# Table steps later in the slot, scatters and fetch ahead of the gathers, adding moved into the next projection

## The chip, the core and the metric

The kernel runs on one core of one Trainium2 chip. A core has five engines that run side by side, each with its own queue of instructions: TensorE (PE) multiplies matrices into PSUM, VectorE (DVE) and ScalarE (ACT) do elementwise work and reductions, GpSimd (POOL) does small operations and issues the indirect transfers here, and SyncE (SP) issues the other transfers. Transfers run on 16 DMA engines that all queues share. The metric is device time in microseconds (us) of one execution; lower is better. Before the change it is 2427.53 us, the median of three runs (2426.61 to 2428.74).

## The reference

32 batches of a 512 x 1024 matrix x go through two layers, each with a residual and a layer norm over the 1024 nodes. Layer 0 is attention over nodes whose score is a sum of two numbers per node, followed by a projection with `adj`; layer 1 multiplies with `adj * adj`.

```python
def _L0_gnn_ref(x, wq, wk, wm, bm):
    q = jnp.einsum('c,bcn->bn', wq, x)
    k = jnp.einsum('c,bcn->bn', wk, x)
    scores = q[:, None, :] + k[:, :, None]
    scores = jnp.where(scores > 0, scores, NEG_SLOPE * scores)
    att = jax.nn.softmax(scores, axis=-1)
    agg = jnp.einsum('bcn,bmn->bcm', x, att)
    out = jnp.einsum('oc,bcm->bom', wm, agg) + bm[None, :, None]
    return jax.nn.relu(out)
...
W = support * kernel
out = jnp.einsum('bnf,nm->bmf', x, W)
out = out + bias
...
x = _layernorm(x + _L0_gnn_ref(x, L0_gnn_wq, L0_gnn_wk, adj, L0_gnn_bm), axis=-1)
x = _layernorm(x + _L1_gnn_ref(x, adj, adj, L1_gnn_bias), axis=-1)
```

(`_L1_gnn_ref` is called with `adj` as both `support` and `kernel`.)

## The kernel before

**The method.** The kernel never forms the 1024 x 1024 attention. exp of a leaky score is exp(q + k) where the sum is positive and exp(0.01 (q + k)) elsewhere. So if the rows z = x^T wm^T are sorted by q, the numerator for one node is one prefix sum and one suffix sum over the sorted rows, each with its weights, cut where q + k changes sign. Per batch b this goes in steps:

- `project(b, nt, part)` (L221, L229): z for 128 nodes at a time into a PSUM tile `zp`, in two halves of eight matmuls each; after the second, ScalarE copies it to `zrow`, of which there is one for all batches. Column 0 of `zrow` is q, the last column k.
- `spread(b)` (L237, L241): q along the free axis in every partition (`qb`, copied to `qs`).
- `place(b, nt)` (L262, L266) on VectorE: the rank of each node by comparing with all q. `send(b, nt)` (L271) on POOL: an indirect transfer that scatters 128 rows of `zrow` to a table `td` in DRAM by rank. `order` is `place` and `send`. There are two tables, one for even and one for odd b.
- `count(b, nt)` (L296) on ScalarE: how many q lie on the positive side for each node; `share(b)` (L304 to L314) makes the row index `idx` and factors from it. `top(b)` (L289, L290) on VectorE: the largest q.
- `fetch(b)` (L324, L329) on SP: eight transfers bring the sorted rows back into `zs`, nine blocks j of two groups of 60 rows. There is one `zs`.
- `weigh(b, part)` (L344 on ScalarE, L349 on VectorE): the weights `w` and the triangular matrices `lw`.
- `table(b, step)`, nine steps (L363 to L377): TensorE makes the prefix sums of one block and the suffix sums of another in the PSUM tile `tp`; ScalarE copies them to `ts` (L368); the last row of each is carried into the next block by a one-row copy, one on POOL (L372) and one on ScalarE (L374), so a step needs the carry of the step before; SP writes the sums to the table `td` (L377).
- `pick(b, mt)` (L391) on POOL: an indirect transfer gathers, for 128 nodes, one row of 3 x 514 floats at `idx` into `g`, of which there is one for all batches.
- `shares` (L411 to L418), `scale` (L427, ScalarE), `gain` (L435, VectorE): the normalised weights, and the weighted sum of the three parts, in place in `g`. The texts call the last two the adding. `shares(b)` without bounds reads all eight gathers.
- `turn(b, ot)` (L470, L474): TensorE transposes the sums to channels by nodes and ScalarE applies bias and relu into `y`; `join` (L481, L444) adds x and makes the statistics on VectorE; `root` (L452, L453) on POOL, `shift` (L459) on VectorE and `apply` (L464) on ScalarE finish the layer norm.
- `layer1(b, mt, h)` (L492): `adj * adj` times `y`; `stats1` (L517, L444) adds the bias and makes statistics; again `root`, `shift`, `apply`; `store` (L522) writes the result. `layer1g` (L507) is the same grouped otherwise, for the first and last batches.

**The order.** The instructions are recorded under a manual schedule: each engine runs its own in the order in which the functions are called, and an instruction that waits holds all behind it in its queue. `begin` and `opening` fill the pipeline, `slot(s)` runs for s = 1 to 29, and `end` empties it. A slot works on four batches: `new` = s + 2 is projected, scattered and fetched; `mid` = s + 1 has its tables made and is gathered; s itself goes through `turn`, `join` and layer 1; `old` = s - 1 is finished and stored.

The slot before has two stages. In eight rounds z = 0 to 7, PE alternates half projections of `new`, table steps of `mid` (two per round, z = 0 to 4) and the transposes of s (z = 1 to 4). The gathers of `mid` are called at z = 4. After `spread(new)` come eight steps h = 0 to 7 of layer 1 of s; beside them VectorE ranks `new` and POOL scatters it (h = 0 to 2), SP fetches it (h = 3), and the adding of `mid` runs from h = 4 into z = 0 of the next slot.

**Buffers.** The PSUM pool `mm` has three tiles of 1024 floats per partition that `zp`, `qb`, `op` (of `turn`) and `o` (of layer 1) share in the order of their calls; `tp` has one tile of its own. `zs`, `g` and `zrow` are single. `ts` has two tiles, `x` twelve (three batches).

Of the kernel before, what the change touches and what calls it, by code (L numbers as in the profile page):

```python
# [23 lines left out]
def gat_gcn_resnorm_kernel(  # L24
# [356 lines left out]
    def bare(b):  # L381

        for i, j in ((0, NB - 1), (1, 0)):
            nc.gpsimd.memset(zs[i * G : i * G + 1, j, 1:ZW], 0.0)

# [164 lines left out]
    def begin():  # L550
# [14 lines left out]
        weigh(0, 0)  # L565
        spread(1)
        weigh(0, 1)
        for z in range(NT):
            project(2, z, 0)
            if 2 * z < NB:  # L570
                table(0, 2 * z)
            if z < NT // 2:
                order(1, 2 * z)
            project(2, z, 1)
            if 2 * z + 1 < NB:
                table(0, 2 * z + 1)
            if z < NT // 2:
                order(1, 2 * z + 1)
            if z == NT // 2:
                bare(0)  # L580
                for mt in range(NT):
                    pick(0, mt)
                top(1)
                fetch(1)
            if z >= NT // 2:
                for nt in (2 * z - NT, 2 * z - NT + 1):
                    count(1, nt)
# [3 lines left out]
    def opening():  # L591

        weigh(1, 0)
        place(2, 0)
        weigh(1, 1)
        table(1, 0)
        table(1, 1)
        place(2, 1)
        shares(0, 0, NT // 2)
        scale(0, range(NT // 2))  # L600
        gain(0, range(NT // 2))
        table(1, 2)
        table(1, 3)
        place(2, 2)
        shares(0, NT // 2, NT)
        scale(0, range(NT // 2, NT))
        gain(0, range(NT // 2, NT))
        table(1, 4)
        table(1, 5)
# [8 lines left out]
        apply(0, 0, CT - 1)  # L618
        for nt in range(NT):
            if nt >= 3:  # L620
                place(2, nt)
            send(2, nt)
            count(2, nt)
        top(2)
        bare(1)
        fetch(2)
        for mt in range(NT):
            pick(1, mt)
# [7 lines left out]
        for mt in range(2):  # L636
            shift(1, 0, mt)
            apply(1, 0, mt)
        weigh(2, 0)
        shares(1)  # L640
        scale(1, range(NT))
        gain(1, range(NT // 2 + 1))

    def slot(s):

        new, mid, old = s + 2, s + 1, s - 1
        for z in range(NT):
            step, ot = 2 * z, z - 1
            project(new, z, 0)
            if step < NB:  # L650
                table(mid, step)
            if 0 < ot < CT:
                root(0, s, ot - 1)
            if z == 0:
                if s > 1:
                    root(1, old, CT - 2)
                weigh(mid, 1)
                gain(s, range(5, NT))
            project(new, z, 1)
            if 0 < ot < CT:  # L660
                turn(s, ot)
            if step + 1 < NB:
                table(mid, step + 1)
            if z == 0:
                stats1(old, CT - 1)
                shift(1, old, CT - 2)
            if ot == 0:
                turn(s, ot)
            if ot == CT - 1:
                for mt in range(3):  # L670
                    pick(mid, mt)
            if z == 1:
                root(1, old, CT - 1)
            if 0 <= ot < CT:
                join(s, ot)
            if z == 1:
                apply(1, old, CT - 2)
                shift(1, old, CT - 1)
            if ot == CT - 1:
                root(0, s, ot)  # L680
                for mt in range(3, NT):
                    pick(mid, mt)
            if ot == CT:
                shift(0, s, CT - 1)
                apply(0, s, CT - 1)
            if z == 2:
                share(mid)
            if z == 3:
                apply(1, old, CT - 1)
            if z < CT:  # L690
                store(old, z)
            if new + 1 < B and 2 <= z < 2 + CT:
                load(new + 1, z - 2)
        spread(new)
        for h in range(CT * NH):
# [9 lines left out]
            if h == 3:  # L705
                fetch(new)
            if h == 4:
                stats1(s, 1)
                root(1, s, 1)
                shares(mid)  # L710
                shift(1, s, 0)
                shift(1, s, 1)
            if h == 5:
                scale(mid, range(NT // 2))
                gain(mid, range(NT // 2))
                apply(1, s, 0)
                apply(1, s, 1)
            if h == 6:
                bare(mid)
                weigh(new, 0)  # L720
            if h == 7:
                scale(mid, range(NT // 2, NT))
                stats1(s, 2)
                gain(mid, [NT // 2])

    def end():

        s, mid, old = B - 2, B - 1, B - 3
        table(mid, 0)
        weigh(mid, 1)  # L730
        gain(s, range(5, NT))
        table(mid, 1)
        root(1, old, CT - 2)
        table(mid, 2)
        stats1(old, CT - 1)
        root(1, old, CT - 1)
        share(mid)
        for ot in range(CT):
            turn(s, ot)
            table(mid, 3 + ot)  # L740
# [4 lines left out]
        shift(1, old, CT - 2)  # L745
        shift(1, old, CT - 1)
        layer1g(s, range(CT - 1), 0)
        table(mid, CT + 3)
        layer1g(s, range(CT - 1), 1)
        table(mid, CT + 4)  # L750
        apply(1, old, CT - 2)
        apply(1, old, CT - 1)
        for mt in range(CT):
            store(old, mt)
        layer1g(s, range(CT - 1), 2)
        layer1g(s, range(CT - 1), 3)
        for mt in range(NT):
            pick(mid, mt)
        for mt in range(CT - 1):
# [73 lines left out]
```

## Time and profile before

| What | Value |
|---|---|
| median of 3 runs | 2427.53 us (2426.61 to 2428.74) |
| the profiled execution | 2426.41 us, span 2424.7 us |
| VectorE busy | 1623.8 us, 67% of the span |
| ScalarE busy | 1472.4 us, 61% |
| POOL busy | 1028.4 us, 42% |
| SP's DMA queue | 276.65 MB, 38.0% of 16 engines' span |
| POOL's DMA queue (scatters and gathers) | 269.52 MB, 29.5% |
| granted TensorE clock | 0.978 mean |

The span is cut by the page into 40 slices. The first rows show each engine's busy share in tenths:

```profile
PE   8965999999999999999999999999999999999975
DVE  3274766677766667766667776666777666777665
PEclk9977999999999999999999999999999999999987
```

A slice is about 61 us. PE is at 9 (90% or more) in all but the first four and the last two. The chain that ended last lies to 74% on PE. In the page's groups a line such as "L492 PE MATMUL o<-y,adj_sb" names the line of the kernel, the engine, the operation and the tiles, written on the left of the arrow and read on its right. In timelines the first number is the start in us, the second the length, and brackets hold the engine's idle time before it and what ended that idle time.

### The profile page before, as it was taken

How to read it: one execution, taken by the hardware profiler on the slowest of the kernel's cores; microseconds unless marked ns; L12 is line 12 of the kernel's file. 1: busy time of each engine (PE TensorE's matmuls, PEld its weight loads, DVE VectorE, ACT ScalarE, POOL GpSimd, SP SyncE). 2: the span in 40 equal slices, each digit the busy share in tenths (PEclk: the TensorE clock that was granted, in tenths of full speed). 3: DMA queues.
4: the chain of work that ended last, by engine and by line, in shares of the span. 5: the costliest groups of instructions: out<-in, count | busy, mean ns of one | idle time of the engine just before them, and what ended most of it. 6: DMA issues, size and time to landing. Idle time of an engine off the chain costs nothing.

```text
span 2424.7 us, 30847 instructions
## 1 busy us (share of the span) xinstructions
PE 2305.3 (95%) x9744; PEld 1441.6 (59%) x9744; DVE 1623.8 (67%) x3250; ACT 1472.4 (61%) x2214; POOL 1028.4 (42%) x1353
## 2 busy tenths in 40 slices
PE   8965999999999999999999999999999999999975
PEld 7633666665666665566666556666566666656532
DVE  3274766677766667766667776666777666777665
ACT  2563666666666756666666656675666666666633
POOL 1432445334444434444533444543444443344431
PEclk9977999999999999999999999999999999999987
DMA  6556776667777666777766777676677776677641
GB/s 239 156 190 194 250 257 246 213 211 235 251 247 257 231 204 222 246 253 248 250 210 218 237 245 252 247 235 205 227 242 259 249 245 209 223 238 250 215 172 69
DMA packets 176835, 548.67 MB, mean 226 GB/s; under 512 B 26304, under 2 KB 26304, under 8 KB 176672
## 3 DMA queue, kind: packets, MB, share of 16 engines
q1 hardware_dynamic: 117600, 276.65, 38.0%
q0 software_dynamic: 57344, 269.52, 29.5%
q8 instruction: 77, 1.26, 0.2%
q14 instruction: 86, 0.70, 0.1%
q10 hardware_dynamic: 1728, 0.53, 0.1%
HBM read 338.17 MB, written 208.43 MB: 225 GB/s over the span
## 4 chain that ended last, share of the span: by engine, by line
PE 74%; DMA 8%; ACT 5%; issue 4%; DVE 4%; POOL 4%; SPq 2%; POOLq 0%; ACTq 0%; DVEq 0%
PE o L492 30%; PE zp L221 26%; PE tp L363 11%; PE op L470 4%; DMA x<-in_x_dram 3%; POOL g L391 2%; PE o L507 2%; DMA g<-td,idx 2%; DMA zs<-td 2%; ACT zrow L229 1%; ACT y L464 1%; SPq L377 1%; ACT v L464 1%; DVE g L435 1%; ACT ts L368 1%
## 5 line engine op out<-in xcount | busy, mean ns | idle before, releaser
L221 PE MATMUL zp<-wmT,x 128*128 128x257 f32 x4096 | 976.5, 388 | 0.0
L221 PEld LDWEIGHTS zp<-wmT,x 128*128 128x128 f32 x4096 | 757.5, 191 | 205.7 <-issue 91.9
L492 PE MATMUL o<-y,adj_sb 128*128 128x512 f32 x1856 | 801.3, 592 | 0.0
L492 PEld LDWEIGHTS o<-y,adj_sb 128*128 128x128 f32 x1856 | 351.8, 191 | 430.0 <-issue 423.1
L372 POOL COPY zs<-ts 1x513 f32<-1x513 f32 x256 | 204.2, 798 | 754.8 <-ACT ts L368 754.5
L435 DVE SCALAR_TENSOR_TENSOR g<-g,ra 128x512 f32<-128x512 f32 x512 | 390.7, 789 | 32.6 <-ACT g L427 23.6
L391 POOL DMA_INDIRECT g<-td,idx x256 | 290.3, 1134 | 271.3 <-DMA x<-in_x_dram 168.7
L363 PE MATMUL tp<-zs,lw 128*64 128x257 f32 x2304 | 325.8, 403 | 57.5 <-POOL zs L372 45.7
L262 DVE SCALAR_TENSOR_TENSOR lt<-qs,zrow,first 128x1024 int8<-128x1024 f32 x256 | 327.8, 1281 | 27.8 <-ACT qs L241 26.8
L271 POOL DMA_INDIRECT td<-zrow,ranki x256 | 273.1, 1067 | 123.3 <-issue 70.8
L296 ACT ACTIVATE sg<-qs,kc 128x1024 int8<-128x1024 f32 x256 | 294.0, 1148 | 7.9
L481 DVE TENSOR_TENSOR y<-y,x 128x1024 f32<-128x1024 f32 x128 | 156.8, 1225 | 177.0 <-ACT y L474 176.8
L464 ACT ACTIVATE y<-y,nb,rs 128x1024 f32<-128x1024 f32 x128 | 158.5, 1238 | 179.7 <-DVE nb L459 178.0
L363 PEld LDWEIGHTS tp<-zs,lw 128*64 128x64 f32 x2304 | 146.4, 139 | 194.2 <-POOL zs L372 94.2
L368 ACT COPY ts<-tp 128x514 f32<-128x514 f32 x288 | 167.9, 583 | 151.1 <-PE tp L363 140.8
L229 ACT COPY zrow<-zp 128x514 f32<-128x514 f32 x256 | 146.7, 584 | 152.1 <-PE zp L221 135.9
L459 DVE SCALAR_TENSOR_TENSOR nb<-mv,rs 128x1 f32<-128x1 f32 x256 | 35.8, 150 | 298.9 <-POOL rs L453 291.7
L414 ACT ACTIVATE ac<-s 128x8 f32<-128x8 f32 (+2 forms) x35 | 7.4, 213 | 290.5 <-DVE s L413 290.5
L427 ACT ACTIVATE g<-g,ra 128x512 f32<-128x512 f32 x256 | 163.5, 710 | 32.2 <-DVE ra L418 32.2
L517 DVE TENSOR_TENSOR v<-o,bias_bc 128x1024 f32<-128x1024 f32 x127 | 154.5, 1217 | 23.6 <-PE o L507 23.1
L464 ACT ACTIVATE v<-v,nb,rs 128x1024 f32<-128x1024 f32 x127 | 152.8, 1227 | 27.3 <-DVE nb L459 27.3
L444 DVE BATCH_NORM_STATS2 st<-y 128x6 f32<-128x512 f32 x256 | 164.7, 685 | 4.4
(75 smaller groups left out, 1641.7 us busy)
## 6 DMA issues: line engine op xcount, KB each, us to landing
x<-in_x_dram SPq DMA_DIRECT2D x128, 512.0 KB
out_dram<-v SPq DMA_DIRECT2D x127, 512.0 KB
td<-ts SPq DMA_DIRECT2D x512, 120.5 KB
zs<-td SPq DMA_DIRECT2D x64, 602.3 KB
zs<-td SPq DMA_DIRECT2D x64, 240.9 KB
zs<-td SPq DMA_DIRECT2D x96, 120.5 KB
td<-ts SPq DMA_DIRECT2D x64, 96.4 KB
td<-zs SPq DMA_DIRECT2D x8, 514.0 KB
```

What stands on the lines that cost most here:

```text
L221: nc.tensor.matmul(zp[:, h, 0:CE], xb[ct][:, nt * P : (nt + 1) * P], wmT[:, ct, h * CE : (h + 1) * CE], start=(ct == 0), stop=(ct == CT - 1),)
L229: nc.scalar.copy(zrow[:, nt, :].rearrange("p (h c) -> p h c", h=2), zps.pop((b, nt))[:, :, 0:CE])
L262: nc.vector.scalar_tensor_tensor(lt, qs, zrow[:, nt, 0:1], first[:, o : o + N], ALU.subtract, ALU.is_lt, accum_out=rank[:, nt : nt + 1],)
L271: sc = nc.gpsimd.indirect_dma_start(out=td[:, :], out_offset=bass.IndirectOffsetOnAxis(ap=ranki[:, nt : nt + 1], axis=0), in_=zrow[:, nt, ...
L296: nc.scalar.activation(sg, qs, AF.Sign, bias=kc[:, nt : nt + 1], accum_out=sgn[:, nt : nt + 1])
L363: nc.tensor.matmul(tp[i * G : (i + 1) * G, h, 0:CE], lt[:, i, j, :], zs[:, j, h * CE : (h + 1) * CE], start=True, stop=True,)
L368: nc.scalar.copy(ts.rearrange("p (h c) -> p h c", h=2), tp[:, :, 0:CE])
L372: nc.gpsimd.tensor_copy(zs[0:1, to, 1:ZW], ts[0:1, 1:ZW])
L391: nc.gpsimd.indirect_dma_start(out=gs[b][:, mt, :], out_offset=None, in_=tds[b].rearrange("(s u) c -> s (u c)", u=3), in_offset=bass.Indir ...
L435: nc.vector.scalar_tensor_tensor(u, g[:, k, i, 1 : C + 1], ra[:, k, i : i + 1], u, ALU.mult, ALU.add)
L464: nc.scalar.activation(t, t, AF.Identity, bias=nb, scale=rs)
L492: nc.tensor.matmul(op[:, h * H : (h + 1) * H], w1[:, ct, mt * P : (mt + 1) * P], yt[ct][:, h * H : (h + 1) * H], start=(ct == 0), stop=(ct ...
```

## The change

The edit touches `begin`, `opening`, `slot` and `end`, and takes out `bare`, which zeroed two carry rows that nothing else writes. No instruction's shape changes; the functions are called in another order.

- **Tables.** In a slot the nine steps of `mid` are called from z = 4 on, two per round, and the ninth after the last projection; `weigh(mid)` is called at z = 2 (before: one part at h = 6 of the slot before, one at z = 0).
- **Gathers.** `pick(mid)` is called at h = 3 of layer 1, after the scatters of `new` and `root(1, s, 0)` on POOL, just ahead of SP's `fetch(new)` in the calls (before: at z = 4, ahead of the scatters).
- **Adding.** `shares`, `scale` and `gain` of s are called at z = 0 to 3 (before: from h = 4 of the slot before to z = 0).
- **Layer norms and stores.** `shift`, `apply`, `store` of `old` move to z = 0 to 2; two `turn`s move to z = 6; two loads of x come after `spread`.
- **Opening and end.** In `opening`, three scatters of batch 2 go ahead of the turns, the gathers of batch 1 ahead of the other five and of the fetch; the adding runs one tile at a time between table steps. `end` follows the same pattern, and the last slot begins the tables of the last batch at h = 6.

The diff, cut to its core:

```diff
-    def bare(b):
-
-        for i, j in ((0, NB - 1), (1, 0)):
-            nc.gpsimd.memset(zs[i * G : i * G + 1, j, 1:ZW], 0.0)
...
     def opening():
...
-        for ot in range(CT):
+        for k in range(NT // 2, NT):
+            scale(0, [k])
+            gain(0, [k])
+            if k % 2:
+                table(1, 2 + k // 2)
+        for nt in range(3):
+            send(2, nt)
+        for ot in range(CT):
             turn(0, ot)
...
         apply(0, 0, CT - 1)
+        for mt in range(NT):
+            pick(1, mt)
+        for nt in range(3, NT):
+            place(2, nt)
+            send(2, nt)
         for nt in range(NT):
-            if nt >= 3:
-                place(2, nt)
-            send(2, nt)
             count(2, nt)
         top(2)
-        bare(1)
         fetch(2)
-        for mt in range(NT):
-            pick(1, mt)
...
     def slot(s):
+        tz = NT // 2
         for z in range(NT):
-            step, ot = 2 * z, z - 1
+            step = 2 * (z - tz)
             project(new, z, 0)
             if z == 0:
                 stats1(old, CT - 1)
+                shares(s)
+                shift(1, old, 1)
+                shift(1, old, 2)
+                scale(s, range(NT // 2))
+            if step >= 0:
+                table(mid, step)
+            if z == 6:
+                root(0, s, 1)
+                turn(s, 2)
+            project(new, z, 1)
+            if z == 0:
+                root(1, old, CT - 1)
+                apply(1, old, 1)
+                gain(s, range(2))
+                store(old, 0)
+                store(old, 1)
             if z == 1:
+                gain(s, range(2, NT // 2))
+                scale(s, range(NT // 2, NT))
+                apply(1, old, 2)
+                store(old, 2)
+            if z == 2:
                 shift(1, old, CT - 1)
+                weigh(mid, 0)
+                weigh(mid, 1)
+                gain(s, range(NT // 2, 6))
+                apply(1, old, CT - 1)
+                store(old, CT - 1)
+            if z == 3:
+                gain(s, range(6, NT))
+                share(mid)
+            if z == 5:
+                root(0, s, 0)
+            if z in (4, 5):
+                turn(s, z - 4)
+            if z == 6:
+                turn(s, 3)
+            if step >= 0:
+                table(mid, step + 1)
+            if z in (4, 5):
+                join(s, z - 4)
+            if z == 6:
+                join(s, 2)
+                root(0, s, 2)
+                join(s, 3)
+                root(0, s, 3)
+            if z == 7:
                 shift(0, s, CT - 1)
                 apply(0, s, CT - 1)
...
+        table(mid, NB - 1)
         spread(new)
+        if new + 1 < B:
+            for ct in (2, 3):
+                load(new + 1, ct)
         for h in range(CT * NH):
             layer1(s, h // NH, h % NH)
...
             if h == 3:
+                for mt in range(NT):
+                    pick(mid, mt)
                 fetch(new)
             if h == 4:
                 stats1(s, 1)
                 root(1, s, 1)
-                shares(mid)
                 shift(1, s, 0)
-                shift(1, s, 1)
-            if h == 5:
-                scale(mid, range(NT // 2))
-                gain(mid, range(NT // 2))
                 apply(1, s, 0)
-                apply(1, s, 1)
             if h == 6:
-                bare(mid)
+                stats1(s, 2)
+                root(1, s, 2)
+            if h == 6 and new == B - 1:
                 weigh(new, 0)
+                weigh(new, 1)
+                table(new, 0)
...
     def end():
...
-        layer1g(s, range(CT - 1), 2)
-        layer1g(s, range(CT - 1), 3)
         for mt in range(NT):
             pick(mid, mt)
+        for ct in range(CT):
+            layer1g(s, range(CT - 1), ct)
```

## The prediction

> **What bounds the kernel now.** First the page's busy row, then the busy time per stretch for three windows of one slot's length, then the timeline of TensorE and VectorE where the program starts.
>
> ```profile
> PE 2305.3 (95%) x9744; PEld 1441.6 (59%) x9744; DVE 1623.8 (67%) x3250; ACT 1472.4 (61%) x2214; POOL 1028.4 (42%) x1353
> ```
>
> ```profile
> 334.00:406.00 72.00, 71.12 (x304) 44.52 (x304) 50.50 (x100) 45.60 (x69) 32.89 (x43) 1.00 0.70 232
> 1000.00:1072.00 72.00, 71.43 (x306) 44.61 (x305) 50.39 (x102) 45.95 (x69) 32.21 (x44) 1.00 0.72 235
> 1800.00:1872.00 72.00, 71.84 (x312) 44.84 (x309) 50.91 (x103) 46.20 (x70) 31.94 (x42) 1.00 0.70 235
> ```
>
> Columns: length, then busy of PE, PEld, DVE, ACT, POOL, then clock, DMA share, GB/s. In the slots PE is busy 71.1 to 71.8 of 72 us at full clock. So nothing can be won in a slot but some tenths; what idles lies in the opening and the end. L492 starts at 262.85 in slot 1 and at 2270.37 in slot 29: (2270.37 - 262.85) / 28 = 71.70 us per slot.
>
> The opening holds one passage in which the order is what the change makes of every slot: the scatters first (POOL 170.7 to 181.9), then fetch and gathers together, then the adding.
>
> ```profile
> 183.09 1.06 POOL L391 DMA_INDIRECT g<-td,idx  x1 [0.16 <-issue]
> ```
>
> ```profile
> 183.69 0.69 SPq L324 DMA_DIRECT2D zs<-td  x2
> 184.42 3.06 SPq L329 DMA_DIRECT2D zs<-td  x6
> ```
>
> ```profile
> 212.85 0.17 DVE L411 TENSOR_TENSOR s<-g,kc 128x8 f32<-128x8 f32 x1 [15.19 <-DMA g<-td,idx]
> ...
> 215.35 7.57 DVE L435 SCALAR_TENSOR_TENSOR g<-g,ra 128x512 f32<-128x512 f32 x10 [0.79 <-ACT g L427]
> 222.84 1.15 DVE L349 TENSOR_TENSOR lw<-tri,w 128x448 f32<-128x448 f32 x2
> 223.91 4.79 DVE L435 SCALAR_TENSOR_TENSOR g<-g,ra 128x512 f32<-128x512 f32 x6
> ```
>
> ```profile
> 220.97 1.98 PE L363 MATMUL tp<-zs,lw 128*64 128x257 f32 x8 [18.04 <-POOL zs L372]
> ```
>
> The reader sees: with fetch and gathers at once, the last gather lands 212.85 - 183.09 = 29.7 us after the first is issued; DVE waits 15.2 us for it and PE 18.0 us. By stretches the DMA share is 1.02 to 1.05 from 188 to 208: the engines are full. In a slot of before it is otherwise: gathers go at 1044.98, land by about 1067, the scatters at 1060 to 1070.6, the fetch at 1073 to 1086, each nearly alone, and L411 finds its gathers there (1071.70, 0.17 us wait).
>
> [...]SP's fetch doesn't wait behind POOL's gathers but shares with them; the trace agrees (29.7 us for both). [...]ScalarE and VectorE run their queues strictly in order, so a waiting instruction holds all behind it; the trace agrees (ACT idle 16.12 us before L414 at 213.46). [...]here L363 takes 1.98 us after the 18 us wait, 1.09 otherwise.
>
> **The change, part by part.** Times from the start of layer 1 (L492) in a slot; before, that stage takes 262.85 to 290.32 = 27.5.
>
> 1. Gathers of `mid`. They move from z = 4 (7 us ahead of layer 1) to h = 3, on POOL behind 8 scatters and root(1,s,0). VectorE sets the pace: places start at 1.24 and come each 1.39 us (1053.58, 1054.98, ...), so 12.4; stats1 to 15.1 (1067.5 - 1052.34); root 0.9: 16.0. First gather about 16.6 (POOL idles 0.3 to 2.7 us between root and gather, 1049.7 to 1052.4). SP's fetch starts at about 15.5 (in the beginning the last scatter goes at 57.83 and SP's fetch at 60.62: 2.8 later). Both together 29.7; 0.7 less as the fetch starts earlier, 1.4 more as store(old,0), 0.5 MB at about 0.37 MB/us, falls in. The last gather lands at L = 47.0. From below: gathers 8 x 128 x 6168 B = 6.32 MB at 381 GB/s (stretch 1061:1066), 16.6 us, and fetch 2.06 MB at 232 (1076:1081), 8.9: 25.5, with 2 us to the first packet 43. From above, a POOL gap of 2.7 and the store in full: 50.5.
> 2. What waits. shares(s) stands in z = 0 on DVE, i.e. at 27.5, and all of g is needed: DVE waits about 17 us. Behind it on ACT stand scale and the copy of zp for z = 0; with three PSUM tiles PE gets through z = 0 to 2 (10.4 us, to 38) and stops. From L: gains start at +2.5 (212.85 to 215.35); 8 of 0.757: +8.55. The next DVE instruction is lw of weigh, whose w is behind scale (4 x 0.64), zrow 0.6, apply 1.24, zrow 0.6, scale 2.56, apply 1.24, zrow 0.6 and 2 pairs of exponentials (0.69 each) on ACT from L + 1.75: +12.5, lw to +13.6. Then 8 gains more: +19.7; the last transpose of turn(s,0): L + 20.2 = 67.2.
> 3. PE from there to the next layer 1: half projection 1.74 us, 1.94 after a table; table 1.02; turn 0.87, 1.02 after a table; qb 1.16. Table 1.02; z = 5 6.79; z = 6 7.61; z = 7 with tables 6, 7 and 8 6.94; qb 1.16: 23.5.
> 4. New waits at the tail. Tables 7 and 8 are neighbours with no projection between; a table frees the next one after ts 0.6 and the POOL row 0.6 (1023.65 to 1025.06): 1.45 idle. And root(0,s,3) stands ahead of table 6's row on POOL and needs join(s,3), while apply(0,s,2) stands ahead of table 6's ts on ACT: from the start of z = 6, relu 7.8, adds and statistics to 12.9, root to 13.85, row 14.5, against 12.5 where PE wants table 7: 2.0. Together 3.5. Half clock after the waits: 2.0.
> 5. Saved in the slot: qb's wait for zrow (0.9) and two half projections after a table (2 x 0.2); both are in 3. bare's two POOL memsets (1.09) were in no chain: nothing. Nor do the other moves count: loads 2 and 3 (1 MB) now stand on SP ahead of the fetch, but run in the first 5 us of layer 1 while VectorE still makes ranks; stores 1 to 3 wait on ACT for the adding and hold only table writes that come later; share, root and shift of layer 1 lie in VectorE's and POOL's idle time. If the gathers were on time, these would still be hidden.
>
> A slot is 67.2 + 23.5 + 3.5 + 2.0 = 96.2: 24.5 more than 71.7, 28 times (slots 2 to 29): +686.
>
> 6. Beginning and opening: PE's waits of 6.49 + 18.04 in slot 1 go, since tables come four projections later; adding in opening runs one by one with scale, without the place between (about 5 us less). But gathers(1) now stand ahead of scatters 3 to 7 and the fetch: scatters at about 176 to 183 behind 6.3 MB, fetch to about 202, the last gains 210, turn(1,0) 211, + 29 = 240 against 262.85. -23.
> 7. End: gathers(30) land 47 us after the last layer 1 begins; half of them serve the first shares, but w of batch 31 needs the fetch (44) and stands ahead on ACT. Gains end at about 63 against 40 (2304.05 + 4.66 - 2270.37 and neighbours): +23. Tables 7 and 8 leave layer1g: -3. Gathers(31) earlier: DVE's stats1 is late there anyway (L411 0.69 us wait): 0. +20.
>
> Sum against the profiled execution, 2426.41 (span 2424.7): 2426 + 686 - 23 + 20 = 3109. The median shown, 2427.53, is 1 us over it: 3110.
>
> **The rivals.** (a) Gathers win against the fetch: alone they took about 19.5 us, so L = 36 and 85.2 a slot: 28 x 13.5 = 378, about 2800. For it: 6168-byte packets move faster than 2056-byte ones; against: the opening, where both ended late. (b) Gathers are hidden and only the tail counts: 74.0 (70.5 of work, 3.5 waits), +2.3: 2427 + 64 - 23 = 2468. Against: gathers would have to land by 27, and POOL can't issue them before 16. (c) The other side, faster: the opening's wait goes and the slots stay full at 71.7, since the nine tables in a row have their rows ready and gathers land in time: 2427 - 23 = 2404. It decides if L is under 27 us and the tail under 0.8 us (23 / 28). For it: that wait is real, 24.5 us; against: 16.6 plus 16.6 us of gather bytes alone is 33. (d) Worse: stores, loads and half clock add 8 us more per slot: 3335.
>
> **How the numbers follow.** Forecast 0.80, (a) 0.09, (b) 0.04, (c) 0.03, (d) 0.04. The unknowns per slot: L -3.8 / +3.5, half clock -2 / +0.5, tail -2 / +1, chain of the adding 0.8; as roots of squares -4.8 / +3.8, so 2975 to 3215. For the cases beside it I take 2900 to 3250. 0.2% is about what a measurement of this kernel tells from no change. Faster 0.03 (c), same 0.01, slower 0.96.
>
> **What would show it.** After: slots of about 96 us; DVE waiting some 17 us at shares for the DMA of g; PE idle some 12 us before the fourth projection (ACT zrow) and again at the transposes (DVE g); DMA share near 1 for some 27 us from the middle of layer 1; tables 7 and 8 waiting for POOL. Wrong if shares starts within 2 us of stats1, or if PE's share stays over 93%.

## The result, and the profile after

The changed kernel takes 3109.79 us (median of 4 runs, 3105.65 to 3110.58) beside 2428.14 us for the kernel before (4 runs): a ratio of 1.280, 95% interval 1.278 to 1.283. The profiled execution has a span of 3108.9 us. First the page of the kernel after: the header, the busy row, TensorE's 40 slices, and one line of the table of groups (busy, mean ns, then the idle time before them and what ended most of it).

```profile
span 3108.9 us, 30419 instructions
...
PE 2449.3 (79%) x9744; PEld 1531.4 (49%) x9744; DVE 1625.5 (52%) x3257; ACT 1466.8 (47%) x2215; POOL 943.1 (30%) x1291
...
PE   8787797777977878877887777887777977779765
...
L221 PE MATMUL zp<-wmT,x 128*128 128x257 f32 x4096 | 1063.3, 416 | 381.0 <-ACT zrow L229 381.0
```

VectorE and ScalarE are busy as long as before (VectorE 1625.5 us against 1623.8), PE runs the same 9744 matmuls, but is busy 144 us longer: in parts of the run its granted clock is 0.5, half of full speed, called half clock below (the mean is 0.887, before 0.978). What is new is above all idle time: from the fifth slice on TensorE is mostly at 7 or 8 tenths where it was at 9. The last line names the largest piece of it: the projection waited 381.0 us for ScalarE's copies of earlier projections.

The slots give the size. Layer 1 (L487 here, L492 before) starts at 242.3 in slot 1 and at 2934.7 in slot 29, so a slot lasts (2934.7 - 242.3) / 28 = 96.16 us, against 71.70 before: 28 x 24.46 = +685. The part up to slot 1 is 20.5 us shorter (262.85 to 242.3), the part from slot 29 on 19.9 longer (154.3 to 174.2). 685 - 20.5 + 19.9 = 684 us, the difference of the spans. Over these 28 slots TensorE is busy 76.19 us of a slot and idle 19.97, before 71.08 and 0.61: of the 24.5 us, 19.4 are idle time and 5.1 work at half clock. About 3 us of the latter lie in projections behind which TensorE waits for the gains anyway (below, 24 matmuls in 8.44 us, where 48 took 10.60).

Where one slot loses its 24 us is read from the timelines of one slot, with layer 1 starting at 1200.46. First POOL, then VectorE and ScalarE:

```profile
1217.17 1.18 POOL L386 DMA_INDIRECT g<-td,idx  x1 [0.57 <-issue]
```

```profile
1247.51 0.17 DVE L406 TENSOR_TENSOR s<-g,kc 128x8 f32<-128x8 f32 x1 [16.59 <-DMA g<-td,idx]
...
1250.01 5.90 DVE L430 SCALAR_TENSOR_TENSOR g<-g,ra 128x512 f32<-128x512 f32 x8 [0.65 <-ACT g L422]
...
1258.29 1.73 DVE L349 TENSOR_TENSOR lw<-tri,w 128x128 f32<-128x128 f32 x4 [2.31 <-ACT w L344]
1259.93 5.89 DVE L430 SCALAR_TENSOR_TENSOR g<-g,ra 128x512 f32<-128x512 f32 x8
```

```profile
1266.28 0.21 ACT L313 ACTIVATE ac<-tk 128x8 f32<-128x8 f32 x1 [5.56 <-DVE tk L308]
...
1266.52 0.57 ACT L368 COPY ts<-tp 128x514 f32<-128x514 f32 x1
```

The first gather is issued 16.7 us after layer 1 began. `shares` begins when the last has landed, 47.05 us after it, and VectorE has stood still for 16.59 us by then. The two rows of gains and the `lw` between them end about 18.3 us later. The ScalarE lines show something the prediction did not have: the exponentials of `share(mid)` (L313) wait 5.56 us for VectorE, and the copy of a table (L368), which PE needs, stands behind them. TensorE in the same slot, from layer 1 to the next:

```profile
1227.93 10.60 PE L221 MATMUL zp<-wmT,x 128*128 128x257 f32 x48
1252.34 8.44 PE L221 MATMUL zp<-wmT,x 128*128 128x257 f32 x24 [13.81 <-ACT zrow L229]
...
1265.88 0.33 PE L465 MATMUL op<-ident,g 128*128 128x128 f32 x1 [1.12 <-DVE g L430]
1267.81 1.24 PE L363 MATMUL tp<-zs,lw 128*64 128x257 f32 x8 [1.61 <-POOL zs L372]
1268.99 3.49 PE L221 MATMUL zp<-wmT,x 128*128 128x257 f32 x8
...
1291.64 1.09 PE L363 MATMUL tp<-zs,lw 128*64 128x257 f32 x8 [1.77 <-POOL zs L372]
1294.09 1.09 PE L363 MATMUL tp<-zs,lw 128*64 128x257 f32 x8 [1.36 <-POOL zs L372]
```

PE gets through three projections, stops for 13.81 us, waits for the gains at the transposes and for the second table, runs one half projection at half clock (3.49 instead of 2.01 us), and waits twice more at the last two tables.

### The profile page after: what moved, and what is told of

Same layout as the page of the kernel before. It is cut to its first block, busy times and chain, and to the rows that moved or that the text cites. A ratio compares the mean times of both kernels' runs of the same rounds, so it can differ in the third digit from the quotient of the medians.

```text
span 3108.9 us, 30419 instructions
## 1 busy us (share of the span) xinstructions
PE 2449.3 (79%) x9744; PEld 1531.4 (49%) x9744; DVE 1625.5 (52%) x3257; ACT 1466.8 (47%) x2215; POOL 943.1 (30%) x1291
## 3 DMA queue, kind: packets, MB, share of 16 engines
q1 hardware_dynamic: 117600, 276.65, 28.2%
## 4 chain that ended last, share of the span: by engine, by line
DMA 23%; issue 20%; PE 20%; DVE 14%; POOL 13%; ACT 9%; POOLq 0%; SPq 0%; ACTq 0%; DVEq 0%
DMA g<-td,idx 19%; PE zp L221 10%; DVE g L430 6%; PE tp L363 6%; POOL td L271 5%; POOL g L386 5%; ACT g L422 3%; PE op L465 3%; DMA td<-zrow,ranki 2%; ACT v L459 2%; POOL zs L372 2%; DVE lw L349 2%; DVE st L439 2%; PE o L502 1%; DMA zs<-td 1%
## 5 line engine op out<-in xcount | busy, mean ns | idle before, releaser
L221 PE MATMUL zp<-wmT,x 128*128 128x257 f32 x4096 | 1063.3, 416 | 381.0 <-ACT zrow L229 381.0
L221 PEld LDWEIGHTS zp<-wmT,x 128*128 128x128 f32 x4096 | 832.4, 208 | 614.9 <-ACT zrow L229 392.3
L487 PE MATMUL o<-y,adj_sb 128*128 128x512 f32 x1856 | 806.7, 595 | 0.0
L372 POOL COPY zs<-ts 1x513 f32<-1x513 f32 x256 | 184.2, 720 | 1532.5 <-ACT ts L368 1532.5
L487 PEld LDWEIGHTS o<-y,adj_sb 128*128 128x128 f32 x1856 | 352.9, 192 | 433.3 <-issue 433.3
L363 PE MATMUL tp<-zs,lw 128*64 128x257 f32 x2304 | 352.5, 430 | 182.9 <-POOL zs L372 172.6
L430 DVE SCALAR_TENSOR_TENSOR g<-g,ra 128x512 f32<-128x512 f32 x512 | 370.5, 755 | 33.4 <-ACT g L422 24.3
L271 POOL DMA_INDIRECT td<-zrow,ranki x256 | 295.2, 1153 | 266.7 <-DVE ranki L266 197.8
L363 PEld LDWEIGHTS tp<-zs,lw 128*64 128x64 f32 x2304 | 153.4, 147 | 330.1 <-POOL zs L372 224.2
L386 POOL DMA_INDIRECT g<-td,idx x256 | 261.1, 1020 | 92.8 <-issue 73.9
L459 ACT ACTIVATE v<-v,nb,rs 128x1024 f32<-128x1024 f32 x127 | 156.7, 1237 | 251.9 <-DVE nb L454 244.1
L368 ACT COPY ts<-tp 128x514 f32<-128x514 f32 x288 | 168.0, 583 | 199.4 <-PE tp L363 188.4
L512 DVE TENSOR_TENSOR v<-o,bias_bc 128x1024 f32<-128x1024 f32 x127 | 155.1, 1221 | 183.7 <-PE o L487 121.5
L465 PE MATMUL op<-ident,g 128*128 128x128 f32 x1024 | 157.4, 287 | 70.9 <-DVE g L430 67.5
L454 DVE SCALAR_TENSOR_TENSOR nb<-mv,rs 128x1 f32<-128x1 f32 x256 | 46.8, 193 | 263.1 <-POOL rs L448 262.9
```

The source lines that it names most:

```text
L221: nc.tensor.matmul(zp[:, h, 0:CE], xb[ct][:, nt * P : (nt + 1) * P], wmT[:, ct, h * CE : (h + 1) * CE], start=(ct == 0), stop=(ct == CT - 1),)
L271: sc = nc.gpsimd.indirect_dma_start(out=td[:, :], out_offset=bass.IndirectOffsetOnAxis(ap=ranki[:, nt : nt + 1], axis=0), in_=zrow[:, nt, ...
L363: nc.tensor.matmul(tp[i * G : (i + 1) * G, h, 0:CE], lt[:, i, j, :], zs[:, j, h * CE : (h + 1) * CE], start=True, stop=True,)
L372: nc.gpsimd.tensor_copy(zs[0:1, to, 1:ZW], ts[0:1, 1:ZW])
L386: nc.gpsimd.indirect_dma_start(out=gs[b][:, mt, :], out_offset=None, in_=tds[b].rearrange("(s u) c -> s (u c)", u=3), in_offset=bass.Indir ...
L430: nc.vector.scalar_tensor_tensor(u, g[:, k, i, 1 : C + 1], ra[:, k, i : i + 1], u, ALU.mult, ALU.add)
```

## The experiments

E4 and E7 are one execution each, without an interval; the others have four or five. Slot lengths, and TensorE's idle and busy time of a slot, are means of the 28 slots of the profiled execution unless something else is said.

**E1. The gathers first.** In the changed kernel, `pick(mid)` goes from h = 3 to h = 0, so ahead of the scatters; nothing else.

```diff
         for h in range(CT * NH):
             layer1(s, h // NH, h % NH)
+            if h == 0:
+                for mt in range(NT):
+                    pick(mid, mt)
...
             if h == 3:
-                for mt in range(NT):
-                    pick(mid, mt)
                 fetch(new)
```

> The changed kernel with the gathers of mid called at h = 0, ahead of the scatters of new on POOL. Theory M (the gathers land 47 us after layer 1 starts, behind the scatters and beside the fetch, and everything of the slot waits for them one for one): the first gather is issued at about 4 us, alone on the DMA engines, and the last lands at about 24 to 27, before the next slot asks for it; the wait of shares (16.6 us) and of PE for zrow (13.8 us) go; what stays is the tail (3.1 us) and some wait for share and for the later fetch, so 75 to 78 us a slot and 2490 to 2590 us in all. Rival R1 (tables late in the projection and the adding beside it are what costs): the slot stays above 90 us, over 2950. Rival R2 (scatters behind 6.3 MB make the fetch late and weigh waits instead): 82 to 90 us a slot, 2700 to 2950, with ScalarE waiting at w for DMA zs.

Measured: 2712.65 us, ratio 1.117 (1.115 to 1.119), about 82 us a slot. So some 14 of the 24.5 us of a slot go with the gathers' place. The rest stays, more than was expected. The size is the one that rival R2 named, but not for its reason: ScalarE doesn't wait for the fetch at `w`. VectorE of one slot, with layer 1 starting at 1060.50:

```profile
1093.26 0.17 DVE L406 TENSOR_TENSOR s<-g,kc 128x8 f32<-128x8 f32 x1 [0.16 <-issue]
...
1095.76 5.89 DVE L430 SCALAR_TENSOR_TENSOR g<-g,ra 128x512 f32<-128x512 f32 x8 [0.65 <-ACT g L422]
...
1105.68 5.89 DVE L430 SCALAR_TENSOR_TENSOR g<-g,ra 128x512 f32<-128x512 f32 x8
```

`shares` no longer waits for a DMA. But it stands on VectorE behind the statistics of layer 1's last two tiles. The last of these can't be made before layer 1 ends (27.6 us), and ahead of both VectorE waits 7.88 us, until 1087.57, for POOL's roots, which stand behind the scatters. So `shares` begins only 32.8 us after layer 1 did. The gains then end at 51 us, while TensorE wants to transpose: `op` waits for them 97.9 us over the run. The tables wait longer still for POOL's carry rows, 157.3 us, the tail's two waits (1.76 and 1.35 us in this slot) among them.

**E2. The root behind the gathers.** `root(1, s, 0)` goes from ahead of the gathers on POOL to behind them.

```diff
-                root(1, s, 0)
...
                     pick(mid, mt)
+                root(1, s, 0)
                 fetch(new)
```

> The changed kernel with root(1, s, 0) behind the gathers on POOL. Theory M: first gather and last landing come 1.0 to 1.5 us earlier (root 0.9 and the gap behind it), and the slot follows one for one: 28 x 1.0 to 1.5 = 28 to 42 us less than 3109.8, so 3068 to 3082. Rival R3 (the fetch, not the gathers, sets when DMA ends, or PE's own work sets the slot): no change, 3105 to 3113.

Measured: 3088.38 us, ratio 1.271 (1.269 to 1.273), 21.4 us less than the changed kernel, where 28 to 42 were expected. The first gather goes 14.7 us after layer 1 begins instead of 16.7, and `shares` begins at 45.6 instead of 47.0 (medians of the slots). So the landing follows the issue, but of 1.4 us per slot only 21.4 / 28 = 0.76 came through. TensorE's idle time falls by 1.36 us a slot, but its busy time rises by 0.62, as more of it runs at half clock: in one slot of its trace the second table takes 1.98 us, at 1262.09, where it took 1.24 in the slot shown above.

**E3. The share early.** `share(mid)` is called at z = 0 rather than behind the gains.

```diff
             if z == 0:
                 stats1(old, CT - 1)
+                share(mid)
                 shares(s)
...
             if z == 3:
                 gain(s, range(6, NT))
-                share(mid)
```

> The changed kernel with share(mid) at z = 0, ahead of shares(s), instead of z = 3 behind the last gain. In the changed kernel the first table's copy to ts waits on ScalarE behind share's exponentials, which wait for VectorE's last gain, and PE then waits 1.61 us at the second table. Theory M': that wait goes and the slot shortens by 1.2 to 1.7 us: 3062 to 3076. Rival: the second table comes after turn(s, 0), which waits for the last gain anyway, so under 0.5 us a slot: 3096 to 3110.

Measured: 3070.93 us (3050.69 to 3084.09), ratio 1.261 (1.257 to 1.266): 38.9 us less by the medians, 1.4 per slot, as expected. Its four executions lie further apart than those of the other kernels, the longest at the lowest granted clock (0.885, the shortest 0.895). In the profiled one, the longest, TensorE is idle 1.51 us less in a slot, of which 0.58 come back as work at half clock; the tail runs at half clock in 15 slots (there `qb` takes 1.97 us instead of 1.09). In a slot of its trace the table starts at once after the last transpose (1254.70 + 0.47, then 1255.10) where it waited 1.61 us before.

**E4. The kernel before with its gathers late.** The gathers of the kernel before go from z = 4 to h = 3 of layer 1, behind the scatters and ahead of the fetch. Tables, adding and norms stay.

```diff
             if ot == CT - 1:
-                for mt in range(3):
-                    pick(mid, mt)
+                pass
...
             if ot == CT - 1:
                 root(0, s, ot)
-                for mt in range(3, NT):
-                    pick(mid, mt)
...
             if h == 3:
+                for mt in range(NT):
+                    pick(mid, mt)
                 fetch(new)
```

> The kernel before with one part of the change alone: its gathers of mid are called at h = 3 behind scatters and root instead of z = 4; tables, adding and all else as before. Theory M: the last gather lands at about 47 us after layer 1 starts, VectorE waits for it at shares in h = 4, lw of the next tables and stats1 stand behind, PE stops at the first table (29 us): 97 to 102 us a slot, 3130 to 3270 in all, so the order of the gathers alone makes the loss. Rival R1 (late tables make it): the gathers are still early enough for the later tables, under 2600.

Measured: 3195.24 us, about 98 us a slot, with no other part of the change in it. From its table of waits (who waited for what, us in total, times, longest; "issue" stands where the profile shows nothing that ended the wait):

```profile
DVE s L411 <- DMA g<-td,idx: 783.4, 31, 29.0
PEld tp L363 <- issue: 781.8, 152, 27.9
PE tp L363 <- issue: 732.7, 30, 27.6
```

In a slot with layer 1 starting at 1145.60, `shares` begins at 1191.46; behind it stand eight gains and the `lw` of the first table (1199.78), and PE, stopped for 25.20 us, starts that table at 1200.16. The place of the gathers alone makes more than the whole loss, 85 us more by this one execution. So with late gathers the changed kernel's other moves, later tables and adding among them, soften the loss. With gathers first (E1) the same moves, in the order that the change gives them, cost some 10 us a slot. The parts don't add up; each is worth what the wait that ends last leaves of it.

**E5. The tail.** E3 with tables one half projection earlier: the first two stand ahead of the first transpose, none are neighbours at the end, and `root(0, s, 3)` goes behind the row of table 7.

```diff
-            step = 2 * (z - tz)
+            step = 2 * (z - tz) + 1
...
-            if step >= 0:
+            if step >= 1:
                 table(mid, step)
+            if z == 7:
+                root(0, s, 3)
...
-            if step >= 0:
+            if step >= -1:
                 table(mid, step + 1)
...
-                root(0, s, 3)
...
-        table(mid, NB - 1)
```

> The changed kernel with share(mid) at z = 0 and the tail mended: the nine tables begin half a round earlier (first one at the end of z = 3), so that a half projection stands between tables 7 and 8, and root(0, s, 3) stands behind table 7's row on POOL. The gathers stay late. Theory: the two tail waits (1.77 and 1.36 us a slot in the changed kernel) go, less what the earlier first table waits for lw: 2 to 3 us a slot under the run with share early alone (3070.9), so 2985 to 3020. Rival: the tail is covered by the wait for ScalarE's last apply, so under 0.7 us a slot: over 3050.

Measured: 2918.13 us, ratio 1.200 (1.198 to 1.202), 89.4 us a slot: 153 us below E3, 5.5 per slot where 2 to 3 were expected. TensorE's idle time falls by 2.76 us a slot, which is what was expected; its busy time falls by another 3.02, which the expectation left out: less work runs at half clock, at the tail in no slot where it did in 15 in E3's trace (`qb` is busy 35.1 us over the run instead of 48.3). Tables 0 and 1 now also fill time in which PE waited for the gains: `op` waits 36.1 us instead of 82.9 over the run.

**E6. Everything read so far in one version.** Gathers at h = 0, the first gains already at h = 7, share early, the tail of E5; the opening stays but for shares and the first gains of batch 1 at its end, and `end` follows suit. The core:

```diff
+            if h == 7:
+                for mt in range(CT - 1):
+                    root(1, s, mt)
+                shares(mid)
+                scale(mid, range(NT // 2))
+                gain(mid, range(2))
+                shift(1, s, 0)
+                apply(1, s, 0)
+                gain(mid, range(2, NT // 2))
...
             if z == 2:
                 shift(1, old, CT - 1)
                 apply(1, old, CT - 1)
                 store(old, CT - 1)
+                weigh(mid, 0)
             if z == 3:
+                table(mid, 0)
+                weigh(mid, 1)
```

> Tables late as in the changed kernel, tail mended, share early, but the gathers of mid first (h = 0) and the adding begun in layer 1 again (shares and half of scale and gain at h = 7, the rest at z = 0 and 1); opening as in the changed kernel. Theory M with the run that had the gathers first: the last gather lands about 24 us after layer 1 starts, gains end at about 43, before PE asks for them at 47; the fetch lands at about 41.5, table 0 needs its first part at 41.4. The slots are then PE's own work, 70.5 to 73 us, the opening keeps its 20 us: 2380 to 2470, about 2400. Rival R1 (late tables and adding in the projection cost of themselves): over 2550.

Measured: 2530.25 us, ratio 1.041 (1.039 to 1.043), 75.7 us a slot: a miss. ScalarE, then TensorE, of a slot of E6:

```profile
1034.08 1.24 ACT L459 ACTIVATE v<-v,nb,rs 128x1024 f32<-128x1024 f32 x1 [2.61 <-DVE nb L454]
1035.22 0.65 ACT L344 ACTIVATE w<-zs,bw,el 128x2 f32<-128x2 f32 x2
```

```profile
1035.98 1.55 PE L363 MATMUL tp<-zs,lw 128*64 128x257 f32 x8 [2.40 <-DVE lw L349]
1037.46 3.45 PE L221 MATMUL zp<-wmT,x 128*128 128x257 f32 x8
```

The weights `w` of the first table (L344) stand behind a normalization (L459) that waits for VectorE, whose instruction for it (`nb`, L454, at 1033.89) stands behind the gains; so the table waits 2.40 us, and the half projection after it runs at half clock (3.45 us instead of 2.01).

**E7. The fetch late.** In the changed kernel `fetch` goes from h = 3 to the projection of the next slot, so that the gathers run without it.

```diff
             if z == 0:
...
+                if s > 1:
+                    fetch(mid)
...
-                fetch(new)
+                if new == B - 1:
+                    fetch(new)
```

> The changed kernel with the fetch of new put off until z = 0 of the next slot, behind store(old, 1), which waits for the adding: the gathers have the DMA engines nearly to themselves, still behind the scatters. Theory: from the first gather's issue to the last landing 21 to 23 us instead of 30, so shares starts at about 39 us after layer 1 instead of 47; but the fetch lands at 57 to 60, lw and with it the second half of the gains wait for it, and the slot keeps 94 to 99 us: 3060 to 3190 in all. Rival (the gathers are slow of themselves, or bound by POOL's issue): landing stays at 28 us or more after the first issue.

Measured: 3125.42 us. What it was made for is in POOL and VectorE of a slot with layer 1 starting at 1198.92, and in the windows of 5 us (length, busy of PE, PEld, DVE, ACT, POOL, clock, DMA share, GB/s):

```profile
1215.64 1.17 POOL L386 DMA_INDIRECT g<-td,idx  x1 [0.58 <-issue]
```

```profile
1237.36 0.17 DVE L406 TENSOR_TENSOR s<-g,kc 128x8 f32<-128x8 f32 x1 [7.98 <-DMA g<-td,idx]
```

```profile
1225.00:1230.00 5.00, 5.00 (x21) 3.73 (x20) 2.72 (x4) 0.00 (x0) 2.85 (x7) 1.00 1.00 414
1230.00:1235.00 5.00, 5.00 (x25) 4.35 (x24) 0.00 (x0) 0.00 (x0) 0.41 (x1) 1.00 1.03 431
```

Alone, the gathers take 21.7 us from the first issue to `shares`, at 38.4 us of the slot; beside the fetch they took 30.3. By this one execution the time of the kernel doesn't fall. In this slot PE's wait for ScalarE shrinks to 5.20 us, but `lw`, whose weights need the fetch, comes only at 1251.02 after 5.20 us of waiting for `w` on VectorE, and holds the second half of the gains, for which the transposes then wait (219.5 us over the run).

**E8. The weights ahead.** E6, with the weights of the first table moved ahead of the last norm of `old`.

```diff
                 store(old, 2)
+                weigh(mid, 0)
                 gain(s, range(6, NT))
-            if z == 2:
-                shift(1, old, CT - 1)
-                apply(1, old, CT - 1)
-                store(old, CT - 1)
-                weigh(mid, 0)
             if z == 3:
                 table(mid, 0)
                 weigh(mid, 1)
+                shift(1, old, CT - 1)
+                apply(1, old, CT - 1)
+                store(old, CT - 1)
```

> The version with gathers first (e6_hybrid, 2530 us, 75.7 us a slot), with one thing moved: weigh(mid, 0) goes from behind the late shift and apply of the old batch (z = 2) to the place behind apply(1, old, 2) in z = 1, ahead of the last two gains; shift and apply of tile 3 go behind weigh(mid, 1) in z = 3. M, what the trace of e6 says: its first table waits 2.4 us for lw, and the half clock after that wait costs 0.46 + 1.44 us more, so 4.2 of 75.7 us; 28 x 4.2 = 118 less, 2400 to 2430 us, below the kernel before; TensorE's wait for lw falls from 105.7 us to under 20. R: the rows of the fetch are not there yet at the earlier place (they land some 4 to 7 us after the issues at 22 to 25 us of the slot), so ScalarE's w waits and holds the copies of the projection behind it: 2500 to 2560 us and a wait of the projection for zrow instead.

Measured: 2391.51 us (2391.31 to 2393.95), ratio 0.984 (0.983 to 0.986): 1.6% less time than the kernel before, and somewhat less than the expected 2400 to 2430. Its page:

```profile
PE 2292.9 (96%) x9744; PEld 1443.3 (60%) x9744; DVE 1612.8 (67%) x3250; ACT 1477.2 (62%) x2214; POOL 972.2 (41%) x1291
...
PE   8979999999999999999999999999999999999775
```

A slot takes 71.05 us (70.9 in most). Beside the kernel before, the slots are 28 x 0.65 = 18 us shorter, the part before slot 1 28.5 shorter (234.3), the part after slot 29 11.9 longer: -35 in the span. TensorE's wait for `lw` fell from 105.7 to 24.4 us over the run.

**E9. The opening alone.** The kernel before, with `begin` and `opening` in the order of the changed kernel and, behind them, the work that the slots of before need done (`weigh(2, 0)`, `shares`, `scale`, five gains of batch 1, two norms).

```diff
+        for mt in range(NT):
+            pick(1, mt)
+        for nt in range(3, NT):
+            place(2, nt)
+            send(2, nt)
...
         fetch(2)
-        for mt in range(NT):
-            pick(1, mt)
```

> The kernel before with begin and opening in the order of the changed kernel (gathers of batch 1 ahead of five scatters and the fetch of batch 2, adding tile by tile between table steps), and with what the slots of before need done ahead of them put behind (two tiles of shift and apply, weigh(2, 0), shares, scale and five gains of batch 1); slots and end as before. M: the forecast's step 6, -23 us, measured -20.5, comes from the opening alone: 2403 to 2412 us, faster than before. R: the 20.5 us were only pushed on (scale and gains of batch 1 left for the first slot), so they come back with the work that the slots of before need done ahead of them: 2420 to 2430 us.

Measured: 2414.9 us, ratio 0.994 (0.992 to 0.995), 15 us less than the kernel before and just above the expected 2403 to 2412. Slot 1 starts at 246.1, 16.8 us earlier than before; 3.7 us come back later. So most of the gain of the opening is real and not pushed on.

**E10. The best version with its gathers behind.** E8, with the gathers of `mid` called at h = 3 as in the changed kernel, the reverse of E1.

> e8_weights_ahead (2391.5 us, 70.9 us a slot) with one thing undone: the gathers of mid are called at h = 3, behind the scatters and ahead of the fetch, as in the changed kernel. M: the last gather lands some 47 us after layer 1 begins; from there the adding (2.5 us to the first gain, two halves of 5.9 us with an lw between) ends at about 66 to 67; two tables can be done before the first turn as in e5_tail (89.4 us a slot); so 88 to 91 us a slot, 28 x 18.5 more: 2870 to 2960 us. R: with tables, weights and adding in the order of e8 the projection has enough other work to cover the later landing, so that half or less of the loss shows: under 2700 us.

Measured: 3009.87 us, ratio 1.239 (1.235 to 1.242); 92.5 us a slot. VectorE, then TensorE, of a slot with layer 1 starting at 1248.16:

```profile
1295.52 0.17 DVE L406 TENSOR_TENSOR s<-g,kc 128x8 f32<-128x8 f32 x1 [23.77 <-DMA g<-td,idx]
```

```profile
1302.88 8.74 PE L221 MATMUL zp<-wmT,x 128*128 128x257 f32 x32 [20.13 <-ACT zrow L229]
```

The expected mechanism, with `shares` at 47.4 us of the slot, but 1.5 us a slot beyond the expected 88 to 91. PE stops after two projections (32 matmuls before the 32 shown), not after three as in the changed kernel. The third of its PSUM tiles still holds the last output of layer 1, whose addition on VectorE (`v<-o`, L512) here stands behind the waiting adding, at 1303.89; this is read from the order of the calls and the two times, and no run moved that addition alone. The one move of the gathers costs 618 us; the whole change cost 682.

## Why the prediction was right, step by step

The mechanism that was forecast is the one that the runs show. That the forecast, 3110 us, and the measured 3109.8 agree so closely is luck all the same: inside a slot two errors of about 1.5 us have opposite signs (step 2), and the mean of 96.16 us is made of five long slots and others of about 95.5 (steps 3 and 4).

**Step 1, the landing of the gathers: right.** Forecast 16.6 us from the start of layer 1 to the first gather and L = 47.0 to the landing of the last; in 28 slots L is 45.9 to 48.9, and 47.05 in the slot shown. The 29.7 us taken from the opening for fetch and gathers together held (30.3). E7 shows that the fetch makes 8 to 9 us of it (21.7 us alone, 30.3 together), E2 that the landing follows the issue; E1, E4 and E10 that the gathers' place is the main cause.

**Step 2, the chain behind the landing: the right mechanism, two sizes off.** From L to the end of the gains the forecast had 19.7 us and the trace 18.3: the `lw` row began at +10.8, not at +12.5. ScalarE's instructions ahead of it follow each other more closely than the sum of their lengths, so the first `w` starts at +10.35 where the forecast's sum gives +11.15; and `lw` begins 0.43 us later, behind the first `w` alone, not behind two pairs of 0.69. In return the forecast had the share out of every chain (step 5, "share, root and shift of layer 1 lie in VectorE's and POOL's idle time"). The trace and E3 show otherwise: ScalarE's part of it waits for VectorE and holds the copy of the first table, 1.61 us at PE in the slot shown, and E3 won 38.9 us by moving it. So 1.4 us too many and 1.6 too few cancel: the second table starts at 67.35, where the forecast had PE resume at 67.2.

**Steps 3 and 4, from there to the next layer 1: nearly right.** In the slot shown, 1296.03 - 1267.81 = 28.2 us against 23.5 + 3.5 + 2.0 = 29.0. The tail's waits are 1.77 + 1.36 = 3.13, not 3.5. E5 shows that they, with the order of tables and transposes, are worth 5.5 us a slot, more than the waits alone, as half clock goes with them (3.02 us less busy time a slot). The forecast has 2.0 us of half clock in step 4, an estimate of its author's, among the tail's waits. In most slots none came there; 1.5 us came earlier, behind the waits at the transposes and the second table. In five slots it also took in the second table and the tail (the last table and `qb` at 1.98 and 1.97 instead of 1.09), and these last 98.3 to 100.3 us. They raise the mean from about 95.5 to 96.16.

**Step 6, the opening: the size right, the reason partly wrong.** Forecast -23, measured -20.5. The forecast let PE's waits go "since tables come four projections later". E9 leaves the tables where they were and still gets 16.8 of it: there the waits before the first two tables shrink together from 24.5 us (6.49 and 18.04) to 13.4 (10.65 and 2.71). The order of gathers, scatters, fetch and adding did most of it, the place of the tables little.

**Step 7, the end:** forecast +20, measured +19.9. In the trace the gains end 64.8 us after layer 1 of slot 29 began (2992.97 + 6.47 - 2934.68), forecast about 63; before they ended after 38.3, taken as 40. No run tested the parts one by one.

**The rivals.** (a), gathers winning against the fetch with L = 36, is out: L is 47, and even with the fetch out of the way it is 38.4. (b), gathers hidden, is out by the 16.59 us wait. (c), faster, asked for L under 27 and an undisturbed tail; E8 reached about that (`shares` starts 24.8 us after layer 1) by putting the gathers first, and took less time than the kernel before, but no run with the gathers behind the scatters comes near. (d), 8 us more per slot from stores, loads and half clock: the five long slots show its mechanism, at 3 to 5 us in one slot out of six.

**What stays open.** The five long slots have the same waits at the tail as the others (1.77 and 1.36 us, in one of the five 2.05 and 1.35). The last section has the clock in one of the five and in one of the others; what sets them apart was not shown. In E5 and E8, where the waits ahead of the tail are gone, no such slot was seen (`qb` is busy 35.1 us over the run in both, 39.5 in the changed kernel). Which of E8's moves, apart from the gathers and the weights, it owes how much was not taken apart either.

## What to carry to other kernels

When a DMA whose result the next stage needs is put behind others on a shared set of DMA engines, price it from a passage of the same trace in which both run together, and follow it to every queue whose head waits for it: here 47 us of landing became 24 us per slot, the largest part of it through ScalarE's copies. Then ask of the other parts of the change whether they cause the loss or soften it. Here late gathers alone lose more than the whole change (E4); the other moves as they stand cost 10 us a slot with early gathers (E1); and late tables with early gathers come out 0.65 us a slot below the kernel before once adding, weights and tail have been placed anew (E8). And a short instruction that waits (the exponentials of 0.21 us, the weights of 0.38 us) costs what stands behind it.

## What the runs showed of the hardware

- **Gathers and fetch together move fewer bytes per second than gathers alone.** The DMA share is 0.96 to 1.04 in both cases, so the engines are full. In E7, without the fetch, the three windows of 5 us from 1220 to 1235 moved 307, 414 and 431 GB/s, 384 in the mean; a store of results was issued just before them, at 1219.45. In the changed kernel, with both, the five windows from 1220 to 1245 moved 307 to 339, 322 in the mean; the fetch alone moved 232 in the kernel before. So the first window of E7 is no faster than those with both, but the next two are. Two windows of the changed kernel, DMA share and GB/s at the end of the line:

```profile
1220.00:1225.00 5.00, 5.00 (x13) 2.17 (x12) 2.72 (x4) 0.96 (x1) 3.94 (x4) 1.00 1.04 309
1230.00:1235.00 5.00, 5.00 (x25) 4.35 (x24) 0.88 (x3) 0.00 (x0) 0.79 (x2) 1.00 1.04 307
```

- **Half clock after short waits.** The two waits at the tail of the changed kernel's slots are 1.77 and 1.35 us, and PE worked 1.09 us between them; in five slots the clock fell there. The last table of the slot that starts at 1296.03, and `qb` behind it, take 1.98 and 1.97 us instead of 1.09:

```profile
1390.18 1.09 PE L363 MATMUL tp<-zs,lw 128*64 128x257 f32 x8 [1.77 <-POOL zs L372]
1392.63 1.98 PE L363 MATMUL tp<-zs,lw 128*64 128x257 f32 x8 [1.35 <-POOL zs L372]
1394.54 1.97 PE L237 MATMUL qb<-ident,zrow 128*128 128x128 f32 x8
```

Below are two stretches of 3.41 us at the tail of the slot that starts at 1200.46: PE is busy for 1.64 and 2.05 us, and the clock, the number behind the five engines' busy times, stays at 1.00. Then two of the next slot: the first contains the whole first wait and the start of the second, PE is busy for 1.41 us, and in the next stretch the clock is 0.50.

```profile
1289.10:1292.51 3.41, 1.64 (x12) 0.83 (x10) 1.62 (x6) 1.28 (x3) 1.35 (x3) 1.00 0.46 170
1292.51:1295.92 3.41, 2.05 (x18) 1.30 (x16) 0.00 (x0) 3.02 (x4) 0.61 (x1) 1.00 0.26 77
...
1388.09:1391.50 3.41, 1.41 (x10) 0.49 (x8) 1.17 (x5) 1.05 (x3) 1.34 (x3) 1.00 0.29 94
1391.50:1394.91 3.41, 2.28 (x10) 1.14 (x11) 0.00 (x0) 2.47 (x4) 0.61 (x1) 0.50 0.24 72
```

The waits are as long in the one slot (1.77 and 1.36 us) as in the other (1.77 and 1.35). So waits of this length can bring half clock and did so in five slots; why not in the others was not shown.
